# Another order of a kernel's beginning, and a common row that is added in a later stage

## The chip, the cores and the metric

The kernel runs on one core of a Trainium2 chip. The time is the device time of one execution in microseconds (us). Three executions before the change took 1510.91, 1511.12 and 1512.03 us; their median, 1511.12, is what the change is measured against.

## The reference, cut to what matters

The program is two layers on x of 2 batches × 2048 tokens × 256 values, all in fp32. Each layer takes a layer norm of x and adds an attention and a feed-forward part of it:

```python
x = L0_attn_x
xn = _layernorm(x)                       # no gain, eps 1e-5
x = x + _L0_attn_ref(xn, ...) + _L0_ffn_ref(xn, ...)
xn = _layernorm(x)
x = x + _L1_attn_ref(xn, ...) + _L1_ffn_ref(xn, ...)
return x

def _L0_attn_ref(x, Wq, bq, Wk, bk, Wv, bv):      # one head of width 256, causal
    q = x @ Wq.T + bq;  k = x @ Wk.T + bk;  v = x @ Wv.T + bv
    return softmax(causal(q @ k.T) / sqrt(256)) @ v

def _L0_ffn_ref(x, gate_w, gate_b, rw1, rb1, ..., sw3, sb3):   # 8 experts, 2 shared ones, hidden 512
    weights, indices = top_k(softmax(x @ gate_w + gate_b), 2)
    routed = sum over the two chosen experts of weight * (silu(x@rw1+rb1) * (x@rw2+rb2)) @ rw3 + rb3
    shared = mean over the two shared experts of (silu(x@sw1+sb1) * (x@sw2+sb2)) @ sw3 + sb3
    return shared + routed

def _L1_attn_ref(x, Wq, Wk, Wv, Wo):              # one head, causal, no biases, output product Wo
    ...
def _L1_ffn_ref(x, ...):       # per batch: a router picks the best of 2048 tokens (k = 256, 255 used);
    ...                        # they alone go through a 16-head attention with rope and a gelu MLP,
                               # and are written back times their router weight; the others pass x through
```

The outputs of layer 0's attention carry the bias bv as a constant row, since the softmax sums to one; the shared experts carry the mean of their two sb3 rows in the same way. The sum of the two is a row of 256 values common to all tokens. The kernel calls it `every`.

## The kernel before

**Tiling.** The 4096 tokens are 8 blocks (g) of 512, four to a batch; a block is an SBUF tile `x_blocks[g]` of 128 partitions × 4 × 256. Attention works on tiles (b, i) of 128 query rows: batch 0 upwards (i = 0 to 15), batch 1 downwards (15 to 0), so that tile (b, i) has i+1 key tiles.

**Stages.** Start-up, to about 32 us; layer 0's attention to 351; routed experts to 704; shared experts to 1122, with the beginning of layer 1's work on batch 0 beside them; layer 1's attention to the end, with the rest of that work beside it.

**Weights of attention.** No keys are projected. With `wa` = Wq·Wkᵀ (L472 to L479, the products in L475) the scores are (xn·wa + ca)·xnᵀ plus a shift for each key or query, so that `ca` (from Wk and bq), a 257th to 265th column of the value weights `wvg` (router weights and Wq·bk) and the single number `qk_bias` = bq·bk stand for the biases. Ten matmuls with one column each make them (L417, L422). To get the products' operands, wq and wk are first transposed on TensorE (L393) and copied by ACT (L394).

**Layer norm.** `moments` (L198) takes mean and variance (bn_stats L205, bn_aggr L206 on DVE), a root by three Newton steps (L182 to L194), and the shift (L214). `layernorm` (L222) normalizes four pieces on ACT (L227), transposes them on TensorE (L233) and copies the result to `xnT[g]` with `evacuate`, which takes DVE and ACT in turn (L154, L156). `prepare0(g)` (L483) does this for layer 0, copies the normalized rows in two halves for the later scatters (POOL, L490), adds `every` to x (POOL, L492), and makes `vg[g]`: values, router logits and key shift of the block (four pairs of products, L499), to which L507 and L508 add the biases.

**Order of the work.** A scheduler reorders the instructions of each engine when the program is built; dependencies are kept, and written-out `order` edges hold an instruction behind another. Around main work a second stream of "side" work is written as Python generators; `beside()` lets it advance `rate` steps at each piece of main work, and `lead()` marks the main instruction behind which a side step's DMAs stand. `HOLD` marks a step whose successor needs data that is still on its way. In layer 0, `side0` (L725) is that stream: moments of blocks 1 to 3, their `prepare0`, moments of 4 to 7, their `prepare0`, routing, 64 scatters of rows to `sorted_x` (L620, from POOL's queue), the first two expert fetches. `before_tile` (L739) steps it until the tile's block has values, and issues DMAs that clear scratch memory from ACT's queue (`clear_some`).

**Attention's inner loop.** Scores L256 on TensorE, a maximum with the shift on DVE (L267), Exp on ACT (L275), a split into two 16-bit halves on POOL (`planes`, L306), a transposing DMA (`across`), copies back to `pT` (L287), the product with values (L321), and x += (L333).

**Routed part** (L803 to L857). A list of tiles of 256 or 128 sorted tokens. For each, SP fetches an expert's three weights, biases and the tokens (a transposing DMA to `xs`); POOL copies the halves to `xT` (L698); TensorE makes two hidden products (L706), ACT the silu, DVE the product `hid` (L821), TensorE the output (L828), DVE adds a bias and SP stores it. xT has three buffers, the copies stand on POOL in tile order.

**Queues.** SP first issues the loads of x's eight blocks, ACT those of wq, wk, bq, bk, wv, the router's weights and ln; POOL those of gate_b, the parts of `every` and router_b.

Of the kernel before, what the change touches and what calls it, by code (L numbers as in the profile page):

```python
# [17 lines left out]
P = 128  # L18
B, S, D = 2, 2048, 256
NB = 8  # L20
# [30 lines left out]
def transformer_kernel(ctx: ExitStack, tc: tile.TileContext, a: dict, out: bass.AP):  # L51
# [27 lines left out]
    for g in range(NB):  # L79
        load_x(g, nc.sync)  # L80
# [69 lines left out]
    def evacuate(dst, src):  # L150

        copies[0] += 1
        if copies[0] % 2:
            nc.vector.tensor_copy(dst, src)  # L154
        else:
            nc.scalar.copy(dst, src)  # L156

    def column(name, n, tag):
        t = const.tile([P, n], F32, tag=tag, name=tag)
        nc.scalar.dma_start(t, a[name])  # L160
        return t
# [36 lines left out]
    def moments(blocks):  # L198

        n = 4 * len(blocks)  # L200
        mv = small.tile([P, 16, 2], F32, tag="ln_mv", name="ln_mv", bufs=2)
        for k, g in enumerate(blocks):
            stats = small.tile([P, 4, 6], F32, tag="ln_stats", name="ln_stats")
            for j in range(4):
                nc.vector.bn_stats(stats[:, j, :], x_blocks[g][:, j, :])  # L205
                nc.vector.bn_aggr(mv[:, 4 * k + j, :], stats[:, j, :])  # L206
            if g != blocks[-1]:
                yield
        var = small.tile([P, 16], F32, tag="ln_var", name="ln_var", bufs=2)
        nc.vector.tensor_scalar(var[:, :n], mv[:, :n, 1], 1e-5, None, op0=ALU.add)  # L210
        rstd = small.tile([P, 16], F32, tag="ln_rstd", name="ln_rstd", bufs=2)
        rsqrt(rstd[:, :n], var[:, :n], n)
        shift = small.tile([P, 16], F32, tag="ln_shift", name="ln_shift", bufs=2)
        nc.vector.scalar_tensor_tensor(  # L214
            shift[:, :n], mv[:, :n, 0], -1.0, rstd[:, :n], op0=ALU.mult, op1=ALU.mult
        )
        for k, g in enumerate(blocks):
            scaled[g] = rstd[:, 4 * k : 4 * k + 4], shift[:, 4 * k : 4 * k + 4]

    scaled = {}  # L220

    def layernorm(g, xn):  # L222

        xb = x_blocks[g]
        rstd, shift = scaled[g]
        for j in range(4):
            nc.scalar.activation(  # L227
                xn[:, j, :D], xb[:, j, :], AF.Identity, bias=shift[:, j : j + 1], scale=rstd[:, j : j + 1]
            )
        for c in range(2):  # L230
            ps = bank("mm")
            for j in range(4):
                nc.tensor.transpose(ps[:, j * P : (j + 1) * P], xn[:, j, c * P : (c + 1) * P], ident)  # L233
            evacuate(xnT[g][:, c, :], ps)
# [143 lines left out]
    with ExitStack() as l0:  # L378
# [6 lines left out]
        wq, wk = (work.tile([P, S], F32, tag="row", name=n)[:, : 2 * D].rearrange("p (c n) -> p c n", c=2)  # L385
                  for n in ("wq", "wk"))
        for dst, name in ((wq, "wq0"), (wk, "wk0")):
            turned = weight(work, name, "qT")
            ps = bank("mm")
            for ec in range(2):  # L390
                for dc in range(2):
                    k = (2 * ec + dc) * P
                    nc.tensor.transpose(ps[:, k : k + P], turned[:, dc, ec * P : (ec + 1) * P], ident)  # L393
            nc.scalar.copy(dst, ps.rearrange("p (c n) -> p c n", c=2))  # L394
        bq = column("bq0", 2, "bq0")
        bk = column("bk0", 2, "bk0")
        wvg = weight(wpool, "wv0", "wvg", cols=D + E + 1)
        nc.scalar.dma_start(wvg[:, :, D : D + E], a["gate_w"].rearrange("(c p) n -> p c n", p=P))
        gate_b = row_broadcast(wpool, ["gate_b"], "gate_b")


        every = wpool.tile([P, 1, D], F32, tag="every", name="every")
        parts = work.tile([P, 4, D], F32, tag="xn", name="parts", bufs=1)
        for k, src in enumerate((a["sb3"][0], a["sb3"][1], a["bv0"])):
            nc.gpsimd.dma_start(parts[:, k, :], src.partition_broadcast(P))
        nc.gpsimd.tensor_tensor(every[:, 0, :], parts[:, 0, :], parts[:, 1, :], ALU.add)
        nc.gpsimd.tensor_scalar(every[:, 0, :], every[:, 0, :], 0.5, None, op0=ALU.mult)
        nc.gpsimd.tensor_tensor(every[:, 0, :], every[:, 0, :], parts[:, 2, :], ALU.add)
        wa = wpool.tile([P, 2, D], F32, tag="wa", name="wa")
        ca = wpool.tile([P, 2], F32, tag="ca", name="ca")  # L410
        qk_bias = wpool.tile([P, 1], F32, tag="qk_bias", name="qk_bias")
        ps = bank("mm")
        for c in range(2):
            at = slice(c * P, (c + 1) * P)
            for k, (w, v) in enumerate(((wk, bq), (wq, bk))):
                for ec in range(2):
                    nc.tensor.matmul(  # L417
                        ps[:, 2 * k + c : 2 * k + c + 1], lhsT=w[:, ec, at], rhs=v[:, ec : ec + 1],
                        start=(ec == 0), stop=(ec == 1),
                    )  # L420
        for ec in range(2):
            nc.tensor.matmul(  # L422
                ps[:, 4:5], lhsT=bq[:, ec : ec + 1].to_broadcast([P, P]), rhs=bk[:, ec : ec + 1],
                start=(ec == 0), stop=(ec == 1),
            )
        nc.vector.tensor_scalar(ca, ps[:, 0:2], 1.0 / 16.0, None, op0=ALU.mult)
        nc.vector.tensor_scalar(wvg[:, :, D + E], ps[:, 2:4], 1.0 / 16.0, None, op0=ALU.mult)
        nc.vector.tensor_scalar(qk_bias, ps[:, 4:5], 1.0 / 16.0, None, op0=ALU.mult)

# [41 lines left out]

        for dc in range(2):  # L472
            ps = bank("mm")
            for ec in range(2):
                nc.tensor.matmul(  # L475
                    ps[:, :D], lhsT=wq[:, ec, dc * P : (dc + 1) * P], rhs=wk[:, ec, :],
                    start=(ec == 0), stop=(ec == 1),
                )
            evacuate(wa[:, dc, :], ps[:, :D])  # L479
        logits = plan.tile([P, NB * 4, E], F32, tag="logits", name="logits")  # L480
        rows, values, shifts = [None] * NB, [None] * NB, [None] * NB

        def prepare0(g):  # L483

            xn = work.tile([P, 4, D], F32, tag="xn", name="xn", bufs=1)
            layernorm(g, xn)
            rows[g] = rows_pool.tile([P, 4, 2 * D], U16, tag=f"rows{g}", name=f"rows{g}")
            halves = xn.bitcast(U16).rearrange("p j (d k) -> p j d k", k=2)
            for k in range(2):
                nc.gpsimd.tensor_copy(rows[g][:, :, k * D : (k + 1) * D], halves[:, :, :, 1 - k])  # L490
            yield
            nc.gpsimd.tensor_tensor(  # L492
                x_blocks[g], x_blocks[g], every[:, 0:1, :].to_broadcast([P, 4, D]), ALU.add
            )
            vg = kv.tile([P, 4, D + E + 1], F32, tag=f"vg{g}", name=f"vg{g}")
            for j in range(4):
                ps = bank("mm")
                for dc in range(2):
                    nc.tensor.matmul(  # L499
                        ps[:, : D + E + 1], lhsT=xnT[g][:, dc, j * P : (j + 1) * P], rhs=wvg[:, dc, :],  # L500
                        start=(dc == 0), stop=(dc == 1),
                    )
                evacuate(vg[:, j, :], ps[:, : D + E + 1])
                yield
            values[g] = vg
            shifts[g] = kv.tile([P, 4], F32, tag=f"shift{g}", name=f"shift{g}")
            nc.vector.tensor_scalar(shifts[g], vg[:, :, D + E], qk_bias, None, op0=ALU.add)  # L507
            nc.vector.tensor_tensor(  # L508
                logits[:, 4 * g : 4 * g + 4, :], vg[:, :, D : D + E],
                gate_b.unsqueeze(1).to_broadcast([P, 4, E]), ALU.add,  # L510
            )

        def route_experts():
# [102 lines left out]
            yield  # L616

# [107 lines left out]
        def side0():  # L725
            for blocks in (range(1, BPB), range(BPB, NB)):
                yield from moments(blocks)
                for g in blocks:
                    yield from prepare0(g)
# [9 lines left out]
        def before_tile(b, i):  # L739
            while values[b * BPB + i // 4] is None:  # L740
                step()
            rate[0] = BESIDE_L0[(values[BPB - 1] is not None) + (values[NB - 1] is not None)]
            if (b, i) > (0, 0):
                clear_some(2 if i < 8 and b == 0 else 1)

        for work_of in (moments([0]), prepare0(0)):
            for _ in work_of:
                pass
# [51 lines left out]
    with ExitStack() as moe:  # L800
        hp = moe.enter_context(tc.tile_pool(name="routed", bufs=2))

        def run(t):  # L803
# [41 lines left out]
        for at, t in enumerate(planned):  # L845
            product, activated = run(t)
            if at >= len(planned) // 3:
# [17 lines left out]
    ln1, ln2 = column("ln1", 2, "ln1"), column("ln2", 2, "ln2")  # L865
# [32 lines left out]
    def prepare(b, rp):  # L898
# [3 lines left out]
        for g in range(b * BPB, (b + 1) * BPB):  # L902
# [4 lines left out]
            elif g == BPB:  # L907
                yield from moments(range(BPB, NB))
# [517 lines left out]
    make_values(sel, 0)  # L1426

# [3 lines left out]
    for g in range(NB):  # L1431
# [15 lines left out]
        for n in range(2):  # L1447
# [19 lines left out]
            for j in range(4):  # L1467
# [11 lines left out]
                if n == 1:  # L1479

                    t = 4 * g + j
                    for rank in range(2):
                        nc.vector.scalar_tensor_tensor(  # L1483
                            xt, found[t, rank], gate[rank][:, t : t + 1], xt, op0=ALU.mult, op1=ALU.add
                        )
                beside()
# [99 lines left out]
```

## Time and profile before

| | us |
|---|---|
| median of three executions | 1511.12 |
| the profiled execution's own time | 1507.24 |
| its span (first to last instruction) | 1505.5 |
| TensorE busy | 1448.6 (96%) |
| VectorE (DVE) busy | 695.7 (46%) |
| ScalarE (ACT) busy | 440.0 (29%) |
| GpSimd (POOL) busy | 407.6 (27%) |
| mean granted TensorE clock | 0.997 of full |

The profile records one execution. PE is TensorE, PEld its weight loads, SP the engine that mainly issues DMAs. A group of instructions is named by its line, engine, operation and tiles (out<-in); in brackets stands the idle time in front of it with what ended it. Windows give each engine's busy time in a stretch of the span. An engine's idle time matters only where that engine sets the pace.

### The profile page before, as it was taken

The page shows a single profiled execution, that of the slowest core. Times are in us where ns is not written, and L with a number is a line of the kernel's source. Part 1 is how long each engine was busy: PE and PEld are TensorE (multiplying, and loading weights), DVE is VectorE, ACT ScalarE, POOL GpSimd, SP SyncE. Part 2 cuts the span into 40 slices and gives each one's busy share as a digit, 9 for nine tenths or more (in the row PEclk, how much of TensorE's full clock was granted, in tenths as well). Part 3 has the DMA queues.
Part 4 walks back from the last instruction along what each step waited for, and adds up shares of the span by engine and source line. Part 5 has one row for each costly group of instructions (what it writes and reads, how often), then busy time and mean ns, then how long its engine had stood idle before and what let it go on. Part 6 is the DMA issues. An engine that isn't in the chain of part 4 may idle for free.

```text
span 1505.5 us, 17837 instructions
## 1 busy us (share of the span) xinstructions
PE 1448.6 (96%) x5796; PEld 1029.9 (68%) x5796; DVE 695.7 (46%) x2068; ACT 440.0 (29%) x831; POOL 407.6 (27%) x597
## 2 busy tenths in 40 slices
PE   6999999999999999999999999999999998999998
PEld 4566666658888888887665656566675765666665
DVE  6347432343222222222424447766546459666344
ACT  2443333332111111111121121115524433344233
POOL 3554776622111111111201221132013122421132
PEclk9999999999999999999999999999999999999999
DMA  5844665685878989873101011220004435621154
GB/s 157 257 115 112 174 149 129 136 162 149 234 221 221 274 234 301 226 208 102 33 21 43 28 43 35 65 97 29 0 14 115 109 70 123 146 51 24 35 119 101
DMA packets 288528, 182.99 MB, mean 122 GB/s; under 512 B 190928, under 2 KB 263376, under 8 KB 288432
## 3 DMA queue, kind: packets, MB, share of 16 engines
q1 hardware_dynamic: 252608, 133.90, 36.4%
q10 hardware_dynamic: 28192, 27.06, 5.7%
q0 software_dynamic: 7632, 20.86, 4.5%
q8 instruction: 48, 0.79, 0.2%
q14 instruction: 48, 0.39, 0.1%
HBM read 93.14 MB, written 45.14 MB: 92 GB/s over the span
## 4 chain that ended last, share of the span: by engine, by line
PE 29%; issue 10%; DVE 7%; POOL 3%; DMA 2%; ACT 2%; POOLq 0%; ACTq 0%; DVEq 0%; SPq 0%
PE ps_tr L1453 6%; PE ps_sc L1453 6%; PE ps_pv L1472 5%; POOL planes L306 3%; DMA across<-planes 2%; PE ps_mm L1324 2%; PE ps_mm L1286 1%; DVE x L1483 1%; PE ps_sc L256 1%; PE ps_mm L916 1%; PE ps_mm L1307 1%; PE ps_pv L321 1%; PE ps_mm L1390 1%; DVE row L267 1%; PE ps_tr L256 1%
## 5 line engine op out<-in xcount | busy, mean ns | idle before, releaser
L306 POOL COPY planes<-row 128x512 uint16<-128x512 uint16 (+3 forms) x320 | 167.1, 567 | 294.3 <-ACT row L275 280.7
L287 ACT COPY pT<-across 128x512 uint16<-128x512 uint16 (+3 forms) x160 | 106.1, 677 | 218.0 <-DMA across<-planes 209.0
L256 PE MATMUL ps_sc<-xnT,qT 128*128 128x512 f32 (+3 forms) x384 | 161.1, 541 | 2.3 <-ACT qT L638 2.2
L1442 POOL DMA_INDIRECT ya<-sorted_y,place x64 | 62.2, 972 | 307.6 <-DVE x L1483 224.7
L821 DVE SCALAR_TENSOR_TENSOR hid<-ps_tr,be,act 128x256 f32<-128x256 f32 (+1 forms) x144 | 60.9, 465 | 180.1 <-PE ps_tr L706 178.8
L820 ACT ACTIVATE act<-ps_sc,be 128x256 f32<-128x256 f32 (+1 forms) x144 | 58.6, 459 | 280.8 <-PE ps_sc L706 280.8
L321 PE MATMUL ps_pv<-v,pT 128*128 128x256 f32 x544 | 128.1, 381 | 5.5 <-ACT pT L287 4.5
L706 PE MATMUL ps_sc<-xT,rw 128*128 128x256 f32 (+1 forms) x576 | 129.6, 368 | 0.6 <-issue 0.6
L706 PE MATMUL ps_tr<-xT,rw 128*128 128x256 f32 (+1 forms) x576 | 129.4, 367 | 0.0
L321 PE MATMUL ps_pv<-vg,pT 128*128 128x256 f32 x544 | 124.5, 380 | 3.6 <-ACT pT L287 3.2
L698 POOL COPY xT<-xs 128x512 uint16<-128x512 uint16 (+1 forms) x72 | 49.1, 727 | 290.7 <-DMA xs<-sorted_x 265.4
L828 PE MATMUL ps_pv<-rw,hid 128*128 128x256 f32 x544 | 124.9, 382 | 0.0
L1453 PE MATMUL ps_sc<-xnT,sw 128*128 128x512 f32 x256 | 121.9, 594 | 1.8 <-PEq L856 1.8
L1453 PE MATMUL ps_tr<-xnT,sw 128*128 128x512 f32 x256 | 122.0, 593 | 0.0
L321 PEld LDWEIGHTS ps_pv<-vg,pT 128*128 128x128 f32 x544 | 101.8, 189 | 26.6 <-ACT pT L287 6.9
L321 PEld LDWEIGHTS ps_pv<-v,pT 128*128 128x128 f32 x544 | 101.3, 189 | 27.3 <-ACT pT L287 8.0
L1472 PE MATMUL ps_pv<-sw,hid 128*128 128x256 f32 x512 | 117.5, 380 | 0.0
L706 PEld LDWEIGHTS ps_sc<-xT,rw 128*128 128x128 f32 x576 | 105.3, 190 | 14.3 <-POOL xT L698 0.9
L706 PEld LDWEIGHTS ps_tr<-xT,rw 128*128 128x128 f32 x576 | 105.1, 190 | 13.2
L828 PEld LDWEIGHTS ps_pv<-rw,hid 128*128 128x128 f32 x544 | 99.2, 190 | 19.3 <-DVE hid L821 5.7
L1472 PEld LDWEIGHTS ps_pv<-sw,hid 128*128 128x128 f32 x512 | 96.6, 190 | 18.8 <-issue 6.2
L256 PEld LDWEIGHTS ps_sc<-xnT,qT 128*128 128x128 f32 x384 | 69.9, 190 | 56.2 <-issue 43.1
(332 smaller groups left out, 1932.2 us busy)
## 6 DMA issues: line engine op xcount, KB each, us to landing
rw<-in_rw SPq DMA_DIRECT2D x108, 512.0 KB, 4.5
sorted_x<-zero ACTq DMA_DIRECT2D x13, 768.0 KB, 6.3
sorted_y<-y SPq DMA_DIRECT2D x32, 256.0 KB, 4.2
be<-biases SPq DMA_DIRECT2D x36, 132.0 KB, 4.1
table<-xn SPq DMA_DIRECT2D x8, 514.0 KB, 3.4
x<-in_x SPq DMA_DIRECT2D x8, 512.0 KB, 6.9
gains<-zero ACTq DMA_DIRECT2D x8, 512.0 KB, 3.6
gain<-gains SPq DMA_DIRECT2D x16, 256.0 KB, 2.6
```

The source lines that it names most:

```text
L256: product = nc.tensor.matmul(ps[:, :w], lhsT=qT[:, dc, (i % 4) * P : (i % 4 + 1) * P], rhs=xnT[g0 + k][:, dc, :w], start=(dc == 0), stop=( ...
L287: nc.scalar.copy(words[:, :, 0], flat[:, w : 2 * w]),
L306: nc.gpsimd.tensor_copy(planes[:, h * w : (h + 1) * w], halves[:, :, 1 - h])
L321: product = nc.tensor.matmul(pv[:, :D], lhsT=turned[k][:, j : j + P], rhs=values[g0 + k][:, j // P, :D], start=(c + j == 0), stop=(c + j = ...
L698: nc.gpsimd.tensor_copy(words[:, :, :, 1 - k], xs[:, 2 * k : 2 * k + 2, :])
L706: product = nc.tensor.matmul(ps[:, k * n : (k + 1) * n], lhsT=we_in[:, dc, (h + k) * P : (h + k + 1) * P], rhs=xT[:, dc, :], start=(dc == ...
L820: activated = nc.scalar.activation(act, p1[:, at], AF.Silu, bias=b1[:, hc])
L821: nc.vector.scalar_tensor_tensor(hid[:, h + k, :], p2[:, at], b2[:, hc], act, op0=ALU.add, op1=ALU.mult)
L828: product = nc.tensor.matmul(po[:, r, :], lhsT=hid[:, hc, r * P : (r + 1) * P], rhs=w3[:, hc, :], start=(hc == 0), stop=(hc == 3),)
L1442: nc.gpsimd.indirect_dma_start(out=ya, out_offset=None, in_=sorted_y, in_offset=bass.IndirectOffsetOnAxis(ap=place[rank][:, t : t + 1], ax ...
L1453: product = nc.tensor.matmul(ps, lhsT=ww[:, dc, hc * P : (hc + 1) * P], rhs=xnT[g][:, dc, :], start=(dc == 0), stop=(dc == 1),)
L1472: product = nc.tensor.matmul(po[:, :D], lhsT=hid[:, hc, j * P : (j + 1) * P], rhs=w["sw3", n][:, hc, :], start=(hc == 0), stop=(hc == 3),)
```

## The change

1. *Loads.* SP loads block 0 of x, then wk, then blocks 1 to 7. ACT's queue keeps wq, wv, the router's weights and ln. POOL's queue takes bk (into an extra column beside wk), bq and gate_b. A dummy Exp on ACT loads the activation table early.
2. *First block.* Its moments come first on DVE, ahead of those of the other blocks, which an `order` edge holds back until its transposed copy; its norm is split between ACT and DVE.
3. *Bias products.* wk's extra column makes Wq·bk a 257th column of the product for `wa`; five one-column matmuls remain (L488 and L492 of the new file); bq·bk joins gate_b in `besides`, added to vg in one operation.
4. *First tiles.* `prepare0(0)` becomes part of the side stream, and `made` counts tiles of values, so that tile (0, i) of attention begins when value tile i exists. Clears begin at tile (0, 4).
5. *Moments a group ahead.* The groups are (1), (2), (3), (4, 5), (6, 7), and each group's moments are written before the norms of the one before it.
6. *The common row.* `every` is loaded and made at the head of the routed part, and added to x in 32 pieces of 128 × 256, one written at each of the last 32 routed tiles. Layer 0's eight adds of 128 × 1024 go.
7. *Scatters.* Six empty steps stand ahead of them in the side stream.
8. *Layer 1.* Mean and variance of blocks 4 to 7 are taken in the loop of the shared experts, right after each tile of x is final.

The diff, cut:

```diff
-    for g in range(NB):
-        load_x(g, nc.sync)
+    load_x(0, nc.sync)
...
-    def moments(blocks):
+    def moments(blocks, mv=None):
         n = 4 * len(blocks)
-        mv = small.tile([P, 16, 2], F32, tag="ln_mv", name="ln_mv", bufs=2)
-        for k, g in enumerate(blocks):
+        met = () if mv is not None else blocks
+        if mv is None:
+            mv = small.tile([P, 16, 2], F32, tag="ln_mv", name="ln_mv", bufs=2)
+        for k, g in enumerate(met):
             for j in range(4):
-                nc.vector.bn_stats(stats[:, j, :], x_blocks[g][:, j, :])
+                i = nc.vector.bn_stats(stats[:, j, :], x_blocks[g][:, j, :])
+                if first:
+                    tc.add_manual_dep(i.ins, first[0].name, order, reason="the first block's norm goes first")
                 nc.vector.bn_aggr(mv[:, 4 * k + j, :], stats[:, j, :])
+                if j == 1 and g >= BPB:
+                    yield HOLD
...
     def layernorm(g, xn):
+        alone = not first
         for j in range(4):
-            nc.scalar.activation(
-                xn[:, j, :D], xb[:, j, :], AF.Identity, bias=shift[:, j : j + 1], scale=rstd[:, j : j + 1]
-            )
+            if alone and j % 2:
+                nc.vector.tensor_scalar(
+                    xn[:, j, :D], xb[:, j, :], rstd[:, j : j + 1], shift[:, j : j + 1], op0=ALU.mult, op1=ALU.add
+                )
+            else:
+                i = nc.scalar.activation(
+                    xn[:, j, :D], xb[:, j, :], AF.Identity, bias=shift[:, j : j + 1], scale=rstd[:, j : j + 1]
+                )
...
+        nc.gpsimd.dma_start(wk[:, :, D], a["bk0"])
+        bq = column("bq0", 2, "bq0", nc.gpsimd)
+        loaded = [weight(work, n, "qT", queue) for n, queue in (("wq0", nc.scalar), ("wk0", nc.sync))]
+        wvg = weight(wpool, "wv0", "wvg", cols=D + E + 1)
+        for g in range(1, NB):
+            load_x(g, nc.sync)
+        nc.scalar.activation(warm, warm, AF.Exp)
+        for _ in moments([0]):
+            pass
...
-        every = wpool.tile([P, 1, D], F32, tag="every", name="every")
...
+                    ps[:, : D + 1], lhsT=wq[:, ec, dc * P : (dc + 1) * P], rhs=wk[:, ec, :],
...
+            nc.vector.tensor_scalar(wvg[:, dc, D + E :], ps[:, D : D + 1], 1.0 / 16.0, None, op0=ALU.mult)
...
         def prepare0(g):
-            nc.gpsimd.tensor_tensor(
-                x_blocks[g], x_blocks[g], every[:, 0:1, :].to_broadcast([P, 4, D]), ALU.add
-            )
...
+                if g == 0:
+                    nc.vector.tensor_tensor(vg[:, j, D:], vg[:, j, D:], besides, ALU.add)
+                    made[0] += 1
                 yield
...
+            yield from quiet(6)
             for t in range(n):
...
         def side0():
-            for blocks in (range(1, BPB), range(BPB, NB)):
-                yield from moments(blocks)
+            yield from prepare0(0)
+            groups = [(1,), (2,), (3,), (4, 5), (6, 7)]
+            yield from moments(groups[0])
+            for k, blocks in enumerate(groups):
+                if k + 1 < len(groups):
+                    yield HOLD
+                    yield from moments(groups[k + 1])
                 for g in blocks:
                     yield from prepare0(g)
...
-            while values[b * BPB + i // 4] is None:
+            while made[0] <= (NB * 4 - 1 if b else i):
                 step()
...
-            if (b, i) > (0, 0):
-                clear_some(2 if i < 8 and b == 0 else 1)
+            if (b, i) >= (0, 4):
+                clear_some(2 if (b, i) < (0, 12) else 1)
...
+        every = hp.tile([P, D], F32, tag="every", name="every", bufs=1)
+        for dst, src in ((parts[:, 0, :], a["sb3"][0]), (parts[:, 1, :], a["sb3"][1]), (every, a["bv0"])):
+            nc.gpsimd.dma_start(dst, src.partition_broadcast(P))
...
             product, activated = run(t)
+            behind_start = at - (len(planned) - NB * 4)
+            if behind_start >= 0:
+                xt = x_blocks[behind_start // 4][:, behind_start % 4, :]
+                nc.gpsimd.tensor_tensor(xt, xt, every, ALU.add)
...
-                yield from moments(range(BPB, NB))
+                yield from moments(range(BPB, NB), mv1)
...
+                    if g >= BPB:
+                        nc.vector.bn_stats(stats[:, j, :], xt)
+                        nc.vector.bn_aggr(mv1[:, t - BPB * 4, :], stats[:, j, :])
```

## The prediction

> **What bounds the kernel now.** I read the busy shares first, then busy time by stage, then the start instruction by instruction, the windows of the granted clock, and the point where attention hands over to the routed experts.
>
> ```profile
> PE 1448.6 (96%) x5796; PEld 1029.9 (68%) x5796; DVE 695.7 (46%) x2068; ACT 440.0 (29%) x831; POOL 407.6 (27%) x597
> ...
> 0.00:32.00 32.00, 19.02 (x68) 13.30 (x69) 22.61 (x139) 8.81 (x16) 11.81 (x27) 1.00 0.56 169
> 32.00:351.00 319.00, 305.56 (x1121) 204.17 (x1120) 139.65 (x460) 121.54 (x206) 178.80 (x251) 0.99 0.63 149
> 351.00:704.00 353.00, 352.42 (x1687) 306.04 (x1685) 85.00 (x182) 60.38 (x147) 47.63 (x72) 1.00 0.81 228
> 704.00:1122.00 418.00, 412.47 (x1487) 260.03 (x1488) 218.46 (x580) 106.95 (x193) 72.38 (x75) 1.00 0.12 38
> 1122.00:1505.50 383.50, 359.15 (x1439) 246.34 (x1437) 230.00 (x709) 142.33 (x270) 97.00 (x173) 1.00 0.39 88
> ```
>
> TensorE (PE) sets the time: the second column minus the third is its idle time, by stage 13.0, 13.4, 0.6, 5.5 and 24.4 us. The change takes away only 5 of some 3,340 PE rows, so it can win idle time and time at half clock, and little else. The start holds 13.0 us in 32.
>
> ```profile
> 5.41 1.09 PE L393 MATMUL ps_mm<-ident,qT 128*128 128x128 f32 x4 [5.41 <-POOL head_of L872]
> 8.99 1.12 PE L393 MATMUL ps_mm<-ident,qT 128*128 128x128 f32 x4 [2.49 <-DMA qT<-in_wk]
> 11.76 1.01 PE L417 MATMUL ps_mm<-bq,wk 128*128 128x1 f32 x4 [1.66 <-ACT wk L394]
> 16.05 2.05 PE L475 MATMUL ps_mm<-wk,wq 128*128 128x256 f32 x4
> ...
> 11.38 0.74 POOL L406 TENSOR_TENSOR every<-parts 128x256 f32<-128x256 f32 x1 [5.50 <-DMA parts<-in_sb]
> 23.51 2.34 POOL L492 TENSOR_TENSOR x<-x,every 128x1024 f32<-128x1024 f32 x1
> 23.83 2.06 DVE L194 SCALAR_TENSOR_TENSOR ln_rstd<-rs_t,rs_y 128x12 f32<-128x12 f32 x1
> 26.75 2.28 PE L499 MATMUL ps_mm<-wvg,xnT 128*128 128x265 f32 x8 [2.06 <-DVE vg L154]
> 28.87 3.60 PE L634 MATMUL ps_mm<-xnT,wa 128*128 128x512 f32 x8
> ```
>
> Columns: start, time, engine, line, work, and in brackets the idle time before and what ended it. The first scores stand behind weights, bias products, all four value products and the query: the query ends at 32.30. L194, normally 0.13 us, takes 2.06 while POOL's L492 runs, and PE waits 2.06 for the copy behind it.
>
> **Part 1, the new start.** wk goes second on SP's queue, behind x0 alone. x0 had landed by 5.61 (the first statistics). wk and wv are 512 KB; at the 349 to 387 GB/s of the windows from 40 to 47 us that is 1.5 us, so wk is there at about 7.1, not 8.99. Its transposes take 1.1 (L393), to 8.2. The wk copy, 0.59 (L394), ends at 8.95: the activation table, 1.28 us in the old path, is now loaded by a dummy Exp while ACT waits for data. bk0 and bq0 come on POOL's queue: the first POOL DMA was issued at 2.34 and moved its packets by about 8.0; at the 7.6 us to landing of the parts DMAs it would be 9.9 and cost 1 us more. L475's four products, 16.05 to 20.06, take 4.0: to 12.9. The 20 records of L417 and L422, 4.43 us, become 10, 2.2: to 15.1. Block 0's norm is ready before: its statistics need 5.61 to 7.4, the root and shift 2.4, and ACT and DVE share the four pieces. Eight transposes at half clock 2.2: 17.3; xnT copied 17.9; the first quarter of the value products (16 records of L499 in 4.3 us, so 1.1) 19.0; the query, L634's 3.60, 22.6 if the clock is up by then as it was at 19.5, 25 if not. The old order reached this state at 32.30, but with the other three quarters of the value products done, 3.2. The lead is 32.3 − 22.6 − 3.2 = **6.5 us** (4 to 8).
>
> Next, from 33 to 130 us, block 1 arrives. Before, PE waited there 1.35, 1.26, 0.67, 1.24, 1.11 and 0.99 us, and the clock fell:
>
> ```profile
> 43.43:46.85 3.42, 1.98 (x10) 0.80 (x8) 0.42 (x3) 2.87 (x6) 0.46 (x1) 1.00 1.09 349
> 46.85:50.27 3.42, 2.77 (x4) 1.23 (x5) 0.66 (x2) 0.89 (x4) 3.42 (x5) 0.50 1.09 313
> 50.27:53.68 3.41, 3.41 (x6) 1.34 (x5) 0.00 (x0) 0.69 (x1) 1.56 (x1) 0.50 1.05 333
> ...
> 47.49 6.75 PE L634 MATMUL ps_mm<-xnT,wa 128*128 128x512 f32 x8 [0.67 <-DVE xnT L154]
> ...
> 1265.39:1268.80 3.41, 1.52 (x4) 0.38 (x2) 3.41 (x8) 0.62 (x1) 3.10 (x6) 1.00 0.83 153
> 1268.80:1272.20 3.40, 1.76 (x8) 0.87 (x9) 3.40 (x6) 0.91 (x2) 0.00 (x0) 1.00 1.02 205
> ```
>
> A row begins with the window's ends, its length and PE's busy time; of its last three numbers the first is the clock (1.00 or 0.50). The same query takes 6.75 instead of 3.60, so 3.1 us are lost. With small gaps the stretch loses 9.4. In the new order each block's statistics stand one group ahead of its norm, and 8 × 2.34 us of L492 no longer stand between the plane copies on POOL or beside the DVE's root chain. I expect 5.5 still lost (about 1 a block from the second on): **3.9 gained**, between 0 and 7. Sum of the start: 10.4, from 5 to 15.
>
> **Part 2, the common row added later.** The 8 adds of 128x1024 (18.7 us of POOL) become 32 of 128x256 at the head of the routed stage. In the built order POOL runs three DMA issues, xT(1), xT(2), three small operations for the row, then all 32 adds in one block, then xT(3). Behind them on POOL stand every later xT copy, and PE waits for those.
>
> ```profile
> 350.75 2.77 POOL L698 COPY xT<-xs 128x512 uint16<-128x512 uint16 x4 [6.70 <-PE ps_pv L321]
> ...
> 363.60 1.43 POOL L698 COPY xT<-xs 128x512 uint16<-128x512 uint16 x2 [9.90 <-DMA xs<-sorted_x]
> ...
> 377.28 1.89 PE L706 MATMUL ps_sc<-xT,rw 128*128 128x256 f32 x8
> ```
>
> xT(3) was ready at 365.0 and wanted at 377.28: 12.3 us of cover. Now: the issues take 1.64 (L405's two in 1.10, bv 0.54), from 350.75 to 352.4, which makes xT(1) late by about 0.5; xT(2) is done at 355.2; the row's three operations (11.38 to 13.89 before) end at 357.9; 32 adds at L406's 0.74, or at 0.70 (between it and a quarter of L492, 0.585), take 22.4 to 23.7; xT(3) follows in 1.43: 381.7 to 383. The stall is 4.0 to 5.2, taken as **4.5**; with 0.585 an add it is 0.3, with the 0.86 of L407 (same shape, one input) 8.5. xT(4) then follows at once and is wanted 10.4 us later, so it is one stall. The adds themselves are hidden.
>
> **The clock after it.** The windows above fell to 0.50 after one with 1.98 of 3.42 busy, for two windows, at 3.1 us; but two with 1.52 and 1.76, a 3.53 us gap across them, kept 1.00. [...] By the row at 43.43 it costs 3.1, by that at 1265.39 nothing. [...]
>
> **Part 3, what is small.** Statistics of blocks 4 to 7 move into the shared loop: 16 × (0.42 + 0.17) = 9.4 us of DVE, in a stage where DVE is busy 218 of 418 us and PE's products are double buffered: 0; without that cover 9.4. The second layer's side work starts three steps earlier, against 24.4 us of PE gaps there: −1 (−3 to +3). Six empty steps put the scatters and the first xT copy one tile later; that copy ended at 320.9 and is wanted at 342.70: 0 (±1). Clears of scratch memory start at the fifth tile and end two tiles later; the bias rows they fill are read once before 351: 0, at most 1. xT(1)'s 0.5 stands.
>
> **Sum** against the profiled execution, 1507.24 (span 1505.5 and 1.7 around it): −10.4 + 4.5 + 1.5 + 0.5 − 1 = −4.9: 1502.3. The median of the runs is 3.9 higher, so **1506**.
>
> **Rivals.** *The gain comes without the bill*: the adds run nearer to 0.6 us, or xT(3) is reached before PE wants it, and the clock stays up. For it: L492's 0.585 a piece; against it: L406's 0.74 for this very shape. −10.4 − 1: about 1499.5.
>
> *The start gain is given back*: the first tiles are short, and each waits for its own softmax, plane copies and transposes, which take as long as before; being early with the scores only lengthens the wait for the next block of x, whose DMAs now queue behind wk. For it: PE's longest waits after 33 us end with xn, xnT and pT, not with weights; against it: the lead is in work that has been done. Gain 5 to 6, bill 4.5 + 1.5 + 0.5 − 1 = 5.5: about 1510.5, no measurable change.
>
> *The block of adds costs more than the start wins*, slower than before: place, POOL between xT(2) and xT(3); price, stall = 32 × t − 18.5 us for t us an add. With the clock's 3 us, the gains of 10.9 (10.4, 1 in the second layer, less xT(1)'s 0.5) are used up at t = 0.83; it is slower by over 0.2% from about 0.92. L407 at 0.86 speaks for it, L406 against. At t = 0.95: 11.9 + 3 − 10.9 = +4, about 1515.
>
> **From this to the numbers.** 0.2%, 3.0 us, is about what a measurement of this kernel can tell from no change. Chances: the forecast 0.45 (its own range 1502.5 to 1509.5), gain without the bill 0.23, gain given back 0.18, slower 0.14. Faster by over 0.2% (under 1508.1): 0.40 of the first, all of the second, 0.02 of the third: 0.65. Slower: 0.12 of the last and 0.01 of the third: 0.13. Same: the rest, 0.22. Range: from 1498 (start gain at 13 and no bill) to 1513.5 (a start gain of 6 with a stall of 7.5); it leaves out about one in ten on each side.
>
> **What would show it.** Right: wk's transposes near 7 to 8 us; first scores near 22 to 25; no 0.50 window between 40 and 60 us; 32 adds in one run on POOL near 358 to 381, an idle of 3 to 6 us on PE in front of tile 3's first product, ended by POOL xT. The prediction is wrong if the adds are spread out between xT copies, if PE's idle time between 20 and 130 us doesn't shrink, or if the second layer's gaps change by over 3 us either way.

## The result: slower by 0.9 per cent, and the profile after

The changed kernel took 1524.38 us (four executions, 1522.89 to 1527.74), the kernel before beside it 1511.57 (1510.91 to 1513.72): a ratio of 1.0092, 95% interval 1.0073 to 1.0110. The forecast was 1506, with a range to 1513.5. It was wrong.

Where the time went is seen best from the moments at which TensorE reaches the same product in both profiles (us from the span's start, read off TensorE's timelines):

| first product of | before | after | difference |
|---|---|---|---|
| layer 0's scores | 32.3 | 20.6 | −11.7 |
| the routed experts | 342.7 | 332.5 | −10.2 |
| the shared experts | 705.8 | 704.3 | −1.5 |
| layer 1's value products | 1140.6 | 1140.1 | −0.5 |
| end of the span | 1505.5 | 1521.2 | +15.7 |

So the start gained what was forecast, the routed part took most of it back (8.7 us; 6.5 were forecast), and layer 1, for which the prediction had a gain of 1, lost 16 between these two profiles. That is about 3 us more than the medians show, 12.8: the profile before is a fast one (1507.24 us). Busy time by stage of the changed kernel, in the columns shown before (the last stage up to its own end):

```profile
0.00:32.00 32.00, 23.29 (x92) 16.37 (x93) 20.92 (x122) 11.08 (x23) 10.48 (x32) 1.00 0.57 164
32.00:351.00 319.00, 302.96 (x1125) 204.34 (x1124) 154.72 (x530) 122.56 (x204) 167.65 (x251) 1.00 0.66 154
351.00:704.00 353.00, 347.04 (x1648) 300.72 (x1646) 83.15 (x177) 56.99 (x140) 64.93 (x96) 0.99 0.80 224
...
1122.00:1521.20 399.20, 367.90 (x1437) 250.48 (x1435) 227.54 (x709) 141.93 (x270) 100.28 (x173) 0.97 0.38 85
```

The columns are the window, its length, busy us of TensorE, its weight loads, DVE, ACT and POOL, then TensorE's clock, DMA share and GB/s. The third row holds 6 us of TensorE idle time where the kernel before had 0.6. In the last row idle time has grown from 24.4 to 31.3 us, and TensorE is busy 8.7 us longer with the same work: its mean granted clock is 0.97 there.

**The start** ran as worked out. The timeline of TensorE in the changed kernel:

```profile
5.76 1.08 PE L422 MATMUL ps_mm<-ident,qT 128*128 128x128 f32 x4 [5.76 <-DMA qT<-in_wq]
7.02 1.11 PE L422 MATMUL ps_mm<-ident,qT 128*128 128x128 f32 x4 [0.17 <-DMA qT<-in_wk]
9.43 3.79 PE L476 MATMUL ps_mm<-wk,wq 128*128 128x257 f32 x8 [1.30 <-ACT wk L423]
14.79 1.07 PE L249 MATMUL ps_mm<-ident,xn 128*128 128x128 f32 x8 [0.41 <-DVE wvg L481]
17.20 3.59 PE L652 MATMUL ps_mm<-xnT,wa 128*128 128x512 f32 x8
```

wk is there at 7.0 (forecast 7.1), the bias products end at 14.4 (forecast 15.1), and the query ends at 20.6, 2 us ahead of the forecast: 0.7 of it by the bias products, 1.1 because the eight transposes at 14.79 took 1.07, at a granted clock of 1.00, and not the 2.2 forecast.

**The block of adds** came as forecast too. POOL, then TensorE, at the head of the routed part:

```profile
342.62 2.80 POOL L716 COPY xT<-xs 128x512 uint16<-128x512 uint16 x4
349.20 21.93 POOL L882 TENSOR_TENSOR x<-x,every 128x256 f32<-128x256 f32 x32
371.07 2.76 POOL L716 COPY xT<-xs 128x512 uint16<-128x512 uint16 x4
...
364.58 3.67 PE L860 MATMUL ps_pv<-rw,hid 128*128 128x256 f32 x16
372.54 3.78 PE L724 MATMUL ps_sc<-xT,rw 128*128 128x256 f32 x8 [4.29 <-POOL xT L716]
376.11 3.14 PE L724 MATMUL ps_tr<-xT,rw 128*128 128x256 f32 x8
```

32 adds take 21.93 us, 0.69 each; TensorE waits 4.29 for xT(3), and its next sixteen matmul records take 6.7 us (372.54 to 379.25). The same sixteen take 3.6 in the run spread_adds below. In stretches of 3.4 us, TensorE is busy 0.00 us in one, and the granted clock is 0.50 in the two behind it:

```profile
368.50:371.90 3.40, 0.00 (x0) 0.00 (x0) 0.47 (x1) 0.00 (x0) 3.40 (x6) 0.99 0.72 177
371.90:375.30 3.40, 2.76 (x7) 2.20 (x8) 0.00 (x0) 0.00 (x0) 1.95 (x4) 0.50 0.46 140
375.30:378.70 3.40, 3.40 (x10) 2.66 (x9) 0.00 (x0) 0.84 (x2) 0.83 (x2) 0.51 0.00 0
```

**Layer 1.** At 1287.3 us the changed kernel is still 1.1 us ahead, with the same score product (1288.4 in the kernel before). From there to the end TensorE's waits, in the view of waits (us in total, times, longest), were in the kernel before

```profile
PE ps_pv L321 <- ACT pT L287: 4.5, 5, 1.4
PE ps_mm L1307 <- ACT pr L1298: 4.5, 4, 1.8
PE ps_mm L1224 <- ACT part L156: 1.2, 1, 1.2
```

and in the changed one

```profile
PE ps_mm L1153 <- issue: 4.8, 1, 4.8
PE ps_mm L1153 <- DVE hn L1173: 4.0, 1, 4.0
PE ps_pv L339 <- DVE pT L304: 3.3, 1, 3.3
PE ps_mm L1343 <- ACT pr L1334: 2.7, 3, 1.8
PE ps_pv L339 <- ACT pT L305: 2.1, 2, 1.4
```

With the smaller ones they add up to 11.6 and 19.5: 7.9 us more. Where the two large waits at L1153 end, the granted clock falls to 0.50 for 6.83 us each (from 1293.40 and from 1406.04), and at two other places for 3.41 each: 20.5 us in all, which is up to 10.2 lost. Together 18, against the 16.8 that are to be explained. Not all of the 10.2 belongs to L1153: one of these two begins at 1395.80, behind a wait of 1.84 us for pr, the other at 1457.24, behind one of 3.31 for pT.

L1153 transposes `hn`, the normalized rows of batch 1's chosen block, which 16 small DVE operations in a row prepare. The view names the first of the two waits "issue", but hn's last operation (L1173) begins on DVE at 1293.60, directly before it ends. TensorE, then DVE:

```profile
1287.33 1.88 PE L274 MATMUL ps_tr<-xnT,qT 128*128 128x512 f32 x4
1294.05 1.28 PE L1153 MATMUL ps_mm<-ident,hn 128*128 128x128 f32 x4 [4.84 <-issue]
...
1289.09 0.46 DVE L304 COPY pT<-across 128x512 uint16<-128x512 uint16 x1 [4.44 <-DMA across<-planes]
1289.50 0.42 DVE L1165 SCALAR_TENSOR_TENSOR hn<-chosen 128x256 f32<-128x256 f32 x1
1293.60 0.77 DVE L1173 TENSOR_SCALAR hn<-chosen,rms_rs 128x256 f32<-128x256 f32 x2
```

The whole chain lies open here. It also began late: the chosen rows' last gather was issued at 1275.9 and such gathers took at most 6.6 us to land, but the chain stands on DVE behind a copy (L304) that waited 4.44 us for its DMA. What another place on DVE would be worth was not tried.

Here is what stands ahead of the second wait, first in the kernel before (L1117), then in the changed one:

```profile
1395.81 3.70 PE L1502 MATMUL ps_mm<-xnT,wqk 128*128 128x512 f32 x8
1399.35 1.97 PE L1363 MATMUL ps_mm<-f_wo,oT 128*128 128x256 f32 x8
1401.15 1.88 PE L256 MATMUL ps_sc<-xnT,qT 128*128 128x512 f32 x4
1402.87 1.88 PE L256 MATMUL ps_tr<-xnT,qT 128*128 128x512 f32 x4
1404.59 1.88 PE L256 MATMUL ps_sc<-xnT,qT 128*128 128x512 f32 x4
1406.49 0.81 PE L1117 MATMUL ps_mm<-ident,hn 128*128 128x128 f32 x4
```

```profile
1400.85 1.99 PE L1399 MATMUL ps_mm<-f_wo,oT 128*128 128x256 f32 x8 [0.88 <-DVE oT L1393]
1406.79 1.16 PE L1153 MATMUL ps_mm<-ident,hn 128*128 128x128 f32 x4 [3.95 <-DVE hn L1173]
1408.53 3.78 PE L1414 MATMUL ps_mm<-hT,xnT 128*128 128x256 f32 x8 [0.57 <-DVE hT L1159]
1412.10 4.22 PE L1543 MATMUL ps_mm<-xnT,wqk 128*128 128x512 f32 x8
```

From the first addition of L1399's result to the end of hn, DVE takes 5.0 us in the changed kernel (1402.02 to 1406.99) and 6.3 in the kernel before (1400.41 to 1406.69), where it does work for the scores in between. Before, three groups of score products lay over it. After, there is no main work left at that place: the query product (L1502 before, L1543 after), which stood ahead of L1363, and the scores that need it come only behind the transposes.

### The profile page after: what moved, and what is told of

The parts are those of the page before. It is cut to its first block, busy times and chain, and to the rows that moved or that the text cites. A ratio compares the mean times of both kernels' runs of the same rounds, so it can differ in the third digit from the quotient of the medians.

```text
span 1521.2 us, 17904 instructions
## 1 busy us (share of the span) xinstructions
PE 1454.2 (96%) x5786; PEld 1032.3 (68%) x5786; DVE 704.2 (46%) x2114; ACT 439.5 (29%) x830; POOL 416.2 (27%) x625
## 5 line engine op out<-in xcount | busy, mean ns | idle before, releaser
L724 PEld LDWEIGHTS ps_sc<-xT,rw 128*128 128x128 f32 x576 | 106.3, 192 | 19.5 <-POOL xT L716 5.7
L304 DVE COPY pT<-across 128x512 uint16<-128x512 uint16 (+3 forms) x160 | 71.9, 456 | 79.7 <-DMA across<-planes 79.1
```

What stands on the lines that cost most here:

```text
L304: nc.vector.tensor_copy(words[:, :, 1], flat[:, :w]),
L724: product = nc.tensor.matmul(ps[:, k * n : (k + 1) * n], lhsT=we_in[:, dc, (h + k) * P : (h + k + 1) * P], rhs=xT[:, dc, :], start=(dc == ...
```

## The experiments

Theory A: part 8 takes three steps from layer 1's side stream, so TensorE's products of batch 1's chosen block come up in its order before their data. Theory B: the earlier start shifts everything against everything. Theory C: the statistics themselves disturb DVE in the shared loop. All ratios are to the kernel before on the same chip. `quiet(n)` stands for n empty steps of the side stream. Times in us are ratios times 1510 unless medians are named.

**late_moments**: part 8 undone; `plain` gives `moments` the yields of the kernel before.

```diff
-                yield from moments(range(BPB, NB), mv1)
+                yield from moments(range(BPB, NB), plain=True)
...
-                    if g >= BPB:
-                        stats = small.tile([P, 4, 6], F32, tag="ln_stats", name="ln_stats")
-                        ...
```

> The changed kernel with part 8 alone undone: mean and variance of blocks 4 to 7 are taken in layer 1's side stream again, which gives it back its three steps. Theory A (the three steps that the side stream lost move its TensorE products in front of data that is not there yet: after 1287 us of the changed kernel's span 16.8 us are lost): 1524.4 - 16.8, about 1508, and the waits for hn near 1290 and 1403 us go. Theory B (the start 10 us earlier shifts transfers and side work against each other, whatever their steps are): stays near 1524. Theory C (the statistics disturb DVE in the shared loop): also 1508, so the next run tells it from A.

Measured: 1.0029 (1.0018 to 1.0040), median 1513.3 against 1509.6. From 1.0092 that is 9.5 us less, and the waits for hn are gone from its profile. The 16.8 were too much to expect. They were counted against a fast profile, and the old order of the side stream has a wait of its own, which comes back: 3.53 us for wrow, here at 1272.42, in the kernel before at

```profile
1270.44 0.25 PE L1071 MATMUL ps_mm<-number,wrow 128*128 128x2 bf16 x4 [3.53 <-DVE wrow L1061]
```

In the changed kernel it is 0.33. So the three steps closed one wait and opened two. The 4.4 us by which this run still lies above the kernel before go with the block of adds, below.

**three_empty_steps**: part 8 kept, the steps given back.

```diff
             elif g == BPB:
+                yield from quiet(3)
                 yield from moments(range(BPB, NB), mv1)
```

> The changed kernel with its statistics in the shared loop kept, and three empty steps in the side stream where the three steps were lost. Theory A: about 1508, like late_moments, within 2 us. Theory B and C: near 1524.

Measured: 1.0033 (1.0021 to 1.0045). The same as late_moments: the steps, not the statistics. Theory C falls. The traces show why the statistics could not matter: in the kernel before, 13 of the 16 for blocks 4 to 7 already ran beside the shared experts (29 records of L205 between 743.6 and 1113.3 us, 16 of them batch 0's), and 13 of 16 do in the changed kernel. DVE is busy 218.5 us in that stage before and 217.9 after.

**before_fold**: the kernel before, with part 8 alone.

```diff
-                yield from moments(range(BPB, NB))
+                yield from moments(range(BPB, NB), mv1)
...
+                    if g >= BPB:
+                        stats = small.tile([P, 4, 6], F32, tag="ln_stats", name="ln_stats")
+                        nc.vector.bn_stats(stats[:, j, :], xt)
+                        nc.vector.bn_aggr(mv1[:, t - BPB * 4, :], stats[:, j, :])
```

> The kernel before with part 8 alone: statistics of blocks 4 to 7 in the shared loop, three side steps fewer. Theory A: 1511.5 + 16, about 1527, with PE waiting for hn near 1290 us. Theory B: 1511, since the start is the old one. Theory C: about 1527 too.

Measured: 1.0082 (1.0055 to 1.0109), 12.4 us. With the old start the same waits stand at the same place, so theory B falls:

```profile
1284.77 1.88 PE L258 MATMUL ps_tr<-xnT,qT 128*128 128x512 f32 x4
1290.98 1.26 PE L1119 MATMUL ps_mm<-ident,hn 128*128 128x128 f32 x4 [4.33 <-issue]
```

**spread_adds**: the block of adds taken apart.

```diff
-                nc.gpsimd.tensor_tensor(xt, xt, every, ALU.add)
+                i = nc.gpsimd.tensor_tensor(xt, xt, every, ALU.add)
+                tc.add_manual_dep(i.ins, turned_x[0].name, order, reason="behind its tile's rows")
```

> The changed kernel with each of the 32 adds of the common row ordered on POOL behind the xT copies of the tile at which it is written. In the changed kernel's trace the block of adds costs a wait of 4.3 us at tile 3, 0.2 around it, and 3.1 us of half clock behind it. If they are due to the block: 1524.4 - 7.6, about 1517, with no wait for xT over 1 us. If the clock or the wait come from elsewhere: 1520 to 1524.

Measured: 1.0060 (1.0035 to 1.0085), 0.3 per cent or 4.8 us below the changed kernel. With five executions the two intervals overlap, so this alone is weak; the same edit made on three_empty_steps (spread_three, next) is clear. In the profile the wait in front of tile 3 is gone, and its products take 1.89 again:

```profile
363.89 3.67 PE L862 MATMUL ps_pv<-rw,hid 128*128 128x256 f32 x16
367.39 1.89 PE L726 MATMUL ps_sc<-xT,rw 128*128 128x256 f32 x8
369.12 1.89 PE L726 MATMUL ps_tr<-xT,rw 128*128 128x256 f32 x8
```

**spread_three** and **spread_six**: spread_adds with three and with six empty steps at the head of layer 1's stream (the edit of three_empty_steps).

> The changed kernel with both edits: three empty steps in layer 1's side stream and the 32 adds each behind its tile's xT copies. three_empty_steps was 1.0033 of the kernel before; spread_adds was 0.3 per cent below the changed kernel. If the two costs add up with the start's gain of 10 us, and layer 1 is then as before: 10 us under the kernel before, a ratio of 0.993 to 0.994. If the half-clock windows in layer 1 (four in three_empty_steps that the kernel before has not, 1.7 us each) come with the order and not with the moment: only 3 to 5 us under, 0.997.

> The same with six empty steps instead of three. If what counts is that data is there when its products come up in TensorE's order, more delay does no harm while the end of the chosen block is covered: within 3 us of spread_three. If the place of three steps is a lucky one: 4 to 10 us slower.

Measured: 0.9984 (0.9974 to 0.9993) and 0.9996 (0.9985 to 1.0007). From three_empty_steps' 1.0033 to 0.9984 are 7.4 us for the block of adds. With both causes removed the kernel is faster than before, but by 3 us (2.4 by the ratio), not by 10. Six steps are 2 us (means) to 3 us (medians) slower than three, barely clear of noise and within the 3 us that were expected if more delay does no harm. But in its profile TensorE waits 5.2 us in front of hn's transposes near 1295 again, so a longer delay doesn't by itself bring cover.

**hold_first**: spread_adds, with the empty steps right in front of hn's transposes.

```diff
         hn = rmsnorm(xs, "hn1")
         yield
+        yield from quiet(3 if b else 0)
         hT = fp.tile([P, 2, TOPK], F32, tag="hT", name="hT1")
         transposed(hn, hT, ln1)
```

> spread_adds with three empty steps put right in front of the transposes of hn in batch 1's chosen block, and none at the head of layer 1's side stream: everything earlier in that stream stays as early as in the changed kernel. If the cost of part 8 is TensorE waiting for hn's chain of some 14 DVE operations without main work in front of it (waits of 4.9 and 4.0 us and the half clock behind each): back to 1505 to 1508, like spread_three. If it lies in the earlier steps of the stream (route, norms): stays at 1515 to 1518.

Measured: 0.9991 (0.9975 to 1.0006), 10 us below spread_adds. All that comes earlier in the side stream is as early as in the changed kernel; only from hn's transposes on is there a delay. At 1288 the wait falls from 4.9 to 1.9 us, at the second place it is gone. This puts the loss where theory A has it: at hn's transposes and what follows them in the stream.

**spread_four**: four empty steps at the head of the stream.

> spread_three with four empty steps instead of three. If any cover in front of hn's products will do: within 3 us of spread_three's 1506.7.

Measured: 0.9980 (0.9969 to 0.9991), 1506.3 against 1510.3: faster than both kernels, and not to be told from spread_three.

**old_start**: spread_three with loads, bias products, first tiles and moments of the kernel before.

```diff
-    load_x(0, nc.sync)
+    for g in range(NB):
+        load_x(g, nc.sync)
...
+        for work_of in (moments([0]), prepare0(0)):   # block 0 whole, ahead of the first tile
+            for _ in work_of:
+                pass
```

> spread_three with the start of the kernel before (loads, bias products, first tiles and moments as they were); parts 6 (spread), 7 and 8 (with its three empty steps) stay. Theory: the new start is worth the 10 us seen at the end of attention in the profiles, so this is 8 to 11 us above spread_three, about 1516. If part of that lead is lost to half-clock windows and waits in layer 1: only 3 to 6 above, about 1511.

Measured: 0.9991 (0.9974 to 1.0009), 1507.2, as good as level with spread_three. A miss for the theory: the new start isn't worth 8 to 11 us, nor, by the means, 3 to 6: it lies 1.3 us above spread_three, give or take 2.

**early_adds**: the other way round, spread_four's start with the eight adds of 128x1024 in layer 0.

```diff
         def prepare0(g):
             ...
             yield
+            nc.gpsimd.tensor_tensor(
+                x_blocks[g], x_blocks[g], every[:, 0:1, :].to_broadcast([P, 4, D]), ALU.add
+            )
```

> spread_four with the common row added in layer 0 again, in eight adds of 128x1024 on POOL right before the value products, as in the kernel before; the new start and the rest stay. In the profile of old_start (old start, adds moved) attention ended 6.5 us earlier than before, in spread_four 8.6 us. If moving the adds is what brings most of the lead: the routed experts begin only 2 to 4 us earlier than before, and the time is 3 to 6 us above spread_four's 1506.3. If the start alone brings the lead, as the prediction had it for the larger part: they begin 7 to 9 us earlier and the time is that of spread_four.

Measured: 1.0011 (0.9999 to 1.0023), 1512.5: 0.31 per cent, or 4.7 us, above spread_four. The moments of four profiles, us from the start:

| first product of | before | old_start | early_adds | spread_four |
|---|---|---|---|---|
| layer 0's scores | 32.3 | 29.9 | 22.0 | 22.3 |
| the routed experts | 342.7 | 336.2 | 339.9 | 334.1 |
| the shared experts | 705.8 | 700.6 | 702.9 | 698.1 |

With the new start alone the lead of 10.3 us at the first scores is 2.8 when the experts begin. With the moved adds alone it is 6.5. These are single profiles: up to the experts, early_adds lost 5.1 us to half clock, before and old_start 3.4, spread_four nothing. The difference of 4.7 in the runs is firmer. One place where it arises is in the timeline of early_adds, while a block's add runs on POOL:

```profile
68.22 2.58 POOL L513 TENSOR_TENSOR x<-x,every 128x1024 f32<-128x1024 f32 x1 [5.78 <-DVE nmx L291]
68.51 2.32 DVE L217 TENSOR_SCALAR ln_var<-ln_mv 128x8 f32<-128x8 f32 x1
74.28 4.54 PE L521 MATMUL ps_mm<-wvg,xnT 128*128 128x265 f32 x12 [3.33 <-DVE xnT L153]
```

An operation on eight columns takes 2.32 us of DVE until POOL's add is through, and TensorE waits 3.33 for the copy of xnT that stands behind it (2.02 at this place in spread_four). Behind the wait its twelve records take 4.54 instead of 3.26, in part at half clock (74.1 to 77.6).

**before_again**: a second profile of the kernel before.

> The kernel before, for a second profile. In its first profile only 5 us were lost to half clock, while its runs beside the experiments lose 8 on the mean (one minus the mean granted clock, times the span). Expected: 6 to 10 us lost, with half-clock windows in layer 1 at the waits near 1270 and 1392 us that the first profile has not.

Its span is 1510.1, with 10.2 us at half clock from 44.8 to 55.1 us and 3.4 behind the wait near 1270, from 1273.6 to 1277.1; near 1392 there is none, though one was expected. It lost about 7.5 us to half clock in all (mean granted clock 0.995), as expected.

## Why the prediction was wrong, by its own steps

By the runs (ratios times 1510, each to the kernel before on its own chip), the miss has two large terms:

| term | forecast | measured | read from |
|---|---|---|---|
| gain of the start and of the moved adds, at the end | −10.4 | −2.4 | spread_three against before |
| block of adds, with the clock and xT(1) | +6.5 | +7.4 | three_empty_steps less spread_three |
| side work three steps earlier | −1 | +8.9 | changed kernel less three_empty_steps |
| sum | −4.9 | +13.9 | (12.8 by the medians) |

**Part 3, "−1 (−3 to +3)" for layer 1's side work three steps earlier: this step failed.** By the runs it measured +9.5 us (late_moments), +9 (three_empty_steps), +12.4 (before_fold, six executions, 8 to 16). The prediction looked at the idle sum of the stage, 24.4 us, and took an earlier stream for a chance to fill it. One gap did close, 3.5 us at wrow. But it didn't look for what covers each of the stream's own chains. At the second place three groups of score products cover hn's chain on DVE in the kernel before; with the stream three steps further on, TensorE's order had none there, and in the profile both uncovered waits were paid twice, once as idle time (4.84 and 3.95 us) and once as half clock behind them (6.83 us each). The prediction reads the built order of POOL, not that of TensorE, in which L1153 stands directly behind L1399. Its own sign of being wrong, gaps of the second layer that change by over 3 us, came true: 24.4 to 31.3.

**Part 1, a lead of 10.4 us by the end of attention: right in size (10.2), wrong in its parts, and wrong as a gain at the end.** It gave 6.5 to the shorter path to the first scores and 3.9 to what follows, with the adds' removal only one of several things in the 3.9. In the two profiles the first part is 8.5 (11.7 less 3.2 of value products still to do). TensorE's idle time from 20 to 130 us hardly shrank, 10.3 to 9.7; what went are the two half-clock windows near 50. In the runs, early_adds and old_start show nearly the reverse of the prediction's shares: about 5 for the adds (early_adds above spread_four), 2 or less for the start (old_start above spread_three and spread_four). The rival of the start gain given back was therefore right about the start alone: early_adds, with a lead of 10 us at the first scores, is 1.0011 of the kernel before. Its mechanism, longer waits for the next block of x, was not tested on its own. Of the whole lead, 3 us are left at the end of spread_three; where the rest goes is taken up in the last paragraph.

**Part 2, a stall of 4.5 at xT(3): right** (4.29; 0.69 an add against 0.70 to 0.74). The 8.5 that it gives for 0.86 an add should be 9.0 by its own formula; nothing rests on it. For xT(1) it had 0.5. A wait of 0.61 for xT stands there, but the kernel before has one of 0.58 at that product; another of 0.73 in front of the first output products is new. Both are in spread_adds too (0.6 and 0.7), so they are not the block's.

**The clock after it: undersized.** 1.5 was taken, 3.1 lost (16 records in 6.7 us instead of 3.6, with the granted clock at 0.50 from 371.80 to 378.63). No run shows the 1.5; the two rows of the kernel before that the prediction cites showed 3.1 and nothing, and the changed kernel showed 3.1, behind a wait that left TensorE 0.00 us busy from 368.50 to 371.90. From the experts' first product to 704 us the measured terms give −10.2 + 4.3 + 3.1 + 0.8 = −2.0, against −1.5 in the table (0.8 is the two waits around xT(1) less the 0.58 of the kernel before).

**Part 3, the rest.** For DVE's 9.4 us in the shared loop it forecast no cost, and there was none, but not for the reason given: 13 of the 16 statistics were there already, so there was next to nothing to hide. The empty steps ahead of the scatters and the shifted clears were not tried alone.

**From the profile to the median.** The prediction put the sum against a profile of 1507.24 and added 3.9. Most of the 3.9 is the clock: that profile lost only 4.0 us to half clock (3.4 from 46.85 to 53.67, 0.6 from 1504.34 to its end), and the kernel's runs lose 8 on the mean.

**Of the rivals**, the slower one named the block of adds. It cost 4.8 us (spread_adds) to 7.4 (spread_three) in the runs and did not decide: without it (spread_adds) the kernel is still 0.6 per cent slower than before.

What stays open is where the lead goes. spread_four is 8 us ahead of before_again when layer 1's value products begin (1133.8 against 1141.8), and 3.6 at the end of the span. It has four half-clock windows in layer 1 where before_again has one (up to 1.7 us each), and a wait of 3.2 us for xnT near 1169; that is more than is lost, so it is no full account, and whether they can be avoided was not tried.

## What to carry to other kernels

Before a stream of side work is moved, list its latency chains on other engines and count the main products that stand over each of them in TensorE's order; the idle sum of the stage doesn't say whether an earlier stream fills gaps or opens them. Empty steps are then a tool: three or four of them in the right place were worth about 9 to 12 us here, and six about 2.5 less than four. A lead in the middle of a kernel is not yet a gain at its end: 10 us at the routed experts were 3 at the end. And work that is moved off an engine can matter through the engine beside it: while one of the adds ran on POOL in layer 0, a small DVE operation took 2.32 us, and TensorE waited 3.33 us for the copy behind it.

## What the runs showed of the hardware that was not expected

**The clock goes with a good part of the spread between runs of one kernel.** In 42 executions of the kernel before on one chip, the time lost to half clock (one minus the mean granted clock, times the span) ran from 3.0 to 12.1 us, and the time followed it with a slope of 0.97 (correlation 0.89). In the three other sets (43, 43 and 27 executions) the slope is 0.90, 0.71 and 0.84 (correlation 0.90, 0.84, 0.86). Up to 1461 us the changed kernel's profile has five stretches at half clock, of 6.83, 6.83, 3.41, 6.83 and 3.41 us, and their ten edges lie on one raster: the first and the last are 1088.85 us apart, 319 times 3.4133, and all ten lie at 3.17 to 3.18 us modulo 3.4133. The four edges of the stretches of 10.2 and 3.4 us in before_again, up to 1277.1 us, lie at 0.46 to 0.49, so the raster stood elsewhere in that execution. The same wait for L1061's wrow (L1097 in late_moments), 3.53 us long, fell differently on it; first the kernel before, then late_moments, with the window after the wait last:

```profile
1265.39:1268.80 3.41, 1.52 (x4) 0.38 (x2) 3.41 (x8) 0.62 (x1) 3.10 (x6) 1.00 0.83 153
1268.80:1272.20 3.40, 1.76 (x8) 0.87 (x9) 3.40 (x6) 0.91 (x2) 0.00 (x0) 1.00 1.02 205
1272.20:1275.60 3.40, 3.40 (x35) 1.86 (x34) 3.40 (x6) 0.47 (x1) 0.00 (x0) 1.00 1.21 201
```

```profile
1267.13:1270.54 3.41, 1.77 (x5) 0.46 (x3) 3.41 (x6) 0.38 (x1) 3.35 (x6) 1.00 0.77 144
1270.54:1273.95 3.41, 1.52 (x8) 0.81 (x9) 3.41 (x7) 1.15 (x2) 0.00 (x0) 1.00 0.95 205
1273.95:1277.36 3.41, 3.41 (x13) 1.48 (x12) 3.41 (x6) 0.00 (x0) 0.00 (x0) 0.50 0.95 191
```

A window with TensorE busy for 1.52 us was followed by full clock in one and by half clock in the other, so the busy time recorded in one window does not decide it here. In late_moments the clock fell to 0.50 though TensorE was busy 1.77 and 1.52 us in the two windows ahead. What does decide it is open.
